# Expert weights queued layer by layer, and a scratch tile taken later, in a graph and mixture-of-experts kernel

## The chip, the cores and the metric

The kernel runs on one core of one Trainium2 chip. The metric is device microseconds for one execution. A core has a matrix engine (TensorE, in the profile PE, with PEld for its weight loads), a vector engine (DVE), a scalar engine (ACT), GpSimd (POOL) and a sync engine (SP) that does nothing here but issue transfers. Transfers run on the core's 16 DMA engines. The engines run side by side and wait for each other by semaphores.

## The reference

Two steps on 1024 nodes of 512 values. The first is a graph layer: normalise, multiply by W, sum over 16384 weighted edges, add a bias, ReLU, add to x. The second is a mixture of 64 experts of which each node takes two, plus a small shared network. Cut to what matters:

```python
x = x + relu(segment_sum(edge_val[:, None] * (layernorm(x) @ W)[edge_col], edge_row) + bias)
xt = layernorm(x)
scores = sigmoid(xt @ Wg.T + bg)
w, idx = top_k(scores, 2);  w = w / w.sum(-1)
cw = zeros(T, E);  cw[t, idx[t]] = w[t]
nx = layernorm(xt)
h = silu(nx @ (gamma*W1) + b1p) * (nx @ (gamma*W3) + b3p)      # per expert, W1 and W3: 512 x 256
y = sum over experts of (h * cw) @ W2 + cw @ b2                # W2: 256 x 512
z = shared network (32 hidden values)
return x + y + z
```

Everything is float32. The weights of one expert are three matrices of 512 KB, so all 64 experts are some 100 MB, and each is read once.

## The kernel before

**The stages.** First comes the graph stage (up to about 170 us): layer norm, product with W, adjacency blocks built from one-hot rows (L402 to L422, L490), their products with the node values (L515), then scores, the choice of two experts per node, and for each expert the list of its nodes (L522 to L629). Then the expert stage: experts are handled in pairs, two blocks of 64 rows side by side. The last part adds results to the nodes and stores them (L1059 to L1086).

**The expert loop** (L999) runs over `order`: 32 pairs, and at index 24 one extra block of 128 rows for an expert that has more than 64 nodes (the index NP in `order`; which expert it is, is known only at run time and read into a register of SP from `oexp_i`). Turn n does, in this order:

- load weights (below); `fetch(n + 4)`: GpSimd gathers the 128 rows of a later pair;
- `hidden` (L771): the first layer, on PE, 8 products over W1 and W3 of both experts (L782, 16 in the trace), then SiLU on ACT (L785) and a multiply on DVE (L787);
- `back(n - 1)`: the second layer of the pair before (`outputs`, L804), copied by ACT and scattered to `y_d` by GpSimd;
- at given turns some side work: at turn 2 `beyond()` (L841), which finds out which experts have more nodes than one block holds; at turns 3 to 11 one-hot rows for the list of the extra blocks (`beyond_hots`, DVE) and, a turn later, their products (`beyond_list`, PE, L910); from turn 6 on, in turns of three, `other_rows` (DVE), `other_turn` (PE) and `other_sum` (PE, DVE) for the shared network and b2;
- `turned` (L794): h is transposed; `front(n + 2)`: the rows of the pair after next are transposed (L194) and scaled (L765, L767).

PE, DVE, ACT, POOL and SP all keep the order in which the program writes their instructions (`manual_schedule`, L988).

**The places for weights.** One pool, `wpool` (L93), has 13 places (AHEAD) of 8 KB a partition under the tag "w13", for W1 and W3 of an expert, and 13 of 4 KB under the tag "w2", for W2. The graph stage uses the same places for its own tiles (`big` and `mid`, L103, L106), and an expert's load waits until the place that it takes is free. Places are handed out as they come free in program order, so that each further W2 takes the place of an earlier W2 or of another tile with that tag. One such other tile is `room` (L843), the scratch of `beyond()`.

**The order on SP's queue.** SP issues loads one after another, and if one must wait, those behind it wait as well. Besides, each load waits for the landing of the load eight before it, so that eight are under way at most. In turns 0 to 2 the loads go expert by expert: W1, W3, W2 (L734, L735, L741). At turn 3 the first layers of experts 6 to 12 are queued together and then their second layers (L1002 to L1006). From expert 13 on it is expert by expert again, except for the last pair, whose first layers precede its second ones (L1011). After all weights, SP loads `ys`, the scattered results, from `y_d` (L1023).

Of the kernel before, what the change touches and what calls it, by code (L numbers as in the profile page):

```python
# [16 lines left out]
ENG = mybir.EngineType  # L17
# [1 line left out]
P = 128  # L19
EPS = 1e-5  # L20
AHEAD = 13
EARLY = 6


@with_exitstack
def kernel(
# [44 lines left out]
    nc = tc.nc  # L71
    N, D = x.shape
    NE = src.shape[0]
    E, _, H = W1.shape
    HS = Ws1.shape[1]
    NT = N // P
# [11 lines left out]
    NP = E // 2  # L88
# [17 lines left out]
    def mid(shape, name, dt, bufs=None):  # L106
        return wpool.tile(shape, dt, name=name, tag="w2")
# [30 lines left out]
    EH = E // 2  # L138
    bias3 = const.tile([3 * EH, 2, 2 * H], BF16, name="bias3")
    picks = const.tile([3 * EH, 2, E], BF16, name="picks")  # L140
# [60 lines left out]
    with tc.tile_pool(name="graph", bufs=1) as gp, \  # L201
# [18 lines left out]
        with tc.manual_schedule(engines={ENG.PE, ENG.DVE, ENG.Activation, ENG.Pool}):  # L220

            nc.gpsimd.iota(iota, pattern=[[1, P]], base=0, channel_multiplier=0, allow_small_or_imprecise_dtypes=True)
            early = mid([P, 8, P], "early", F32)
# [507 lines left out]
    def load_first(queue, w1_of, w3_of):  # L731

        w13 = wpool.tile([P, 2, KC, H], F32, name="w13", tag="w13")
        queue.dma_start(w13[:, 0], w1_of.rearrange("o (p k) h -> p (o k) h", k=KC))  # L734
        queue.dma_start(w13[:, 1], w3_of.rearrange("o (p k) h -> p (o k) h", k=KC))  # L735
        return w13

    def load_second(queue, w2_of):

        w2 = wpool.tile([P, HC, D], F32, name="w2", tag="w2")  # L740
        queue.dma_start(w2, w2_of.rearrange("o (p c) d -> p (o c) d", c=HC))  # L741
        return w2

    def load_expert(queue, w1_of, w3_of, w2_of):
        return load_first(queue, w1_of, w3_of), load_second(queue, w2_of)
# [77 lines left out]
    either = {a: pick_o[:, a, :] for a in range(2)}  # L823
    novf_i = const.tile([1, 1], I32, name="novf_i")
    oexp_i = const.tile([1, NOVF], I32, name="oexp_i")
# [69 lines left out]
    def beyond_hots(c):  # L895

        hots = []
        for n in range(2):
            so = bp.tile([P, P], F32, name="oso", bufs=2)
            nc.vector.tensor_scalar(so, rank_at, oslot[:, c, n:n + 1], None, op0=ALU.is_equal)  # L900
            bo = bp.tile([P, NOVF], F32, name="obo", bufs=2)
            nc.vector.tensor_scalar(bo, iota[:, :NOVF], block[:, c, n:n + 1], numb[:, c, n:n + 1],
                                    op0=ALU.is_equal, op1=ALU.mult)
            hots.append((so, bo))
        return hots
# [7 lines left out]
    def beyond_lists():  # L913
        nc.vector.tensor_copy(lists_o, found)
        nc.vector.tensor_scalar(tokens_o, lists_o, 1, None, op0=ALU.logical_shift_right)
# [51 lines left out]
    order = list(range(NP))  # L967
    order.insert(NP - 8, NP)
    LAST = NP
    xTs, hTs = {}, {}  # L970

    def fetch(n):
        if n < len(order):
            q = order[n]
            gather(rows_of[n % NR], tokens[:, q:q + 1] if q < NP else tokens_o[:, 0:1])

    def front(n):
        if n < len(order):
            q = order[n]
            g, b = (gT[:, :, 2 * q:2 * q + 2], bT[:, :, 2 * q:2 * q + 2]) if q < NP else (g_o, b_o)  # L980
            xTs[n] = scaled(rows_of[n % NR], g, b)

    def back(n):
        if n >= 0:
            q = order[n]
            scatter(outputs(*hTs.pop(n)), lists[:, q:q + 1] if q < NP else lists_o[:, 0:1])

    with tc.manual_schedule(engines={ENG.PE, ENG.DVE, ENG.Activation, ENG.Pool, ENG.SP}):  # L988
        for rows in rows_of:
            nc.scalar.activation(rows, ones[:, 0:1].to_broadcast([P, D]), AF.Copy, scale=0.0)  # L990
        for n in range(NR):
            fetch(n)
        front(0)
        fetch(NR)
        front(1)

        hots, st, sT = None, None, None
        loaded = {}
        for n, q in enumerate(order):  # L999
            if q < NP:  # L1000
                both = (2 * q, 2 * q + 1)
                if n == EARLY // 2:  # L1002

                    early = range(EARLY, AHEAD)
                    firsts = [load_first(nc.sync, W1[e:e + 1], W3[e:e + 1]) for e in early]
                    loaded = {e: (w13, load_second(nc.sync, W2[e:e + 1])) for e, w13 in zip(early, firsts)}  # L1006
                if n < LAST:
                    experts = [loaded.pop(e) if e in loaded else
                               load_expert(nc.sync, W1[e:e + 1], W3[e:e + 1], W2[e:e + 1]) for e in both]
                else:  # L1010
                    experts = list(zip([load_first(nc.sync, W1[e:e + 1], W3[e:e + 1]) for e in both],  # L1011
                                       [load_second(nc.sync, W2[e:e + 1]) for e in both]))
                parts = [(of, {e // EH: picks[:, e // EH, e:e + 1]}) for of, e in zip(experts, both)]
            else:
                e = nc.values_load(oexp_i[0:1, 0:1], engines=[ENG.SP], min_val=0, max_val=E - 1)
                parts = [(load_expert(nc.sync, W1[ds(e, 1)], W3[ds(e, 1)], W2[ds(e, 1)]), either)]
            fetch(n + 4)
            if n == LAST:

                y_of = y_d.rearrange("(i p n) d -> i p n d", p=P, n=2)  # L1020
                ys = [wpool.tile([P, 2, 2, D], F32, name="ys", tag="w13")[:, j] for i in range(NT // 2) for j in range(2)]
                for i in range(NT):
                    nc.sync.dma_start(ys[i], y_of[i])  # L1023
                hots_last = [block_hots(tokens[:, NP - 2 + m:NP - 1 + m], w_last[m]) for m in range(2)]
                diag = wpool.tile([P, 2, P], F32, name="diag", tag="w2")
                for j in range(2):
                    nc.scalar.activation(diag[:, j, :], ident, AF.Copy, scale=wts[:, NT - 2 + j, 1:2])
            h = hidden(xTs.pop(n), parts)
            if n < LAST:
                back(n - 1)  # L1030
            else:
                y_last = [outputs(*hTs.pop(LAST - 1))]
            if n == 0:
                weights()
            if n == 2:
                beyond()
            if 4 <= n < 4 + NT:
                beyond_list(hots)
            if 3 <= n < 3 + NT:
                hots = beyond_hots(n - 3)  # L1040
            if n == 4 + NT:
                beyond_lists()

            if n >= 6 and (n - 6) // 3 < NT:
                i = (n - 6) // 3
                if n % 3 == 0:
                    st = other_rows(i)
                elif n % 3 == 1:
                    sT = other_turn(st)
                else:  # L1050
                    other_sum(i, sT)
            if n == LAST - 2:
                w_last = [block_weights(lists[:, NP - 2 + m:NP - 1 + m]) for m in range(2)]
            hTs[n] = (turned(h), parts)
            front(n + 2)

        pos = {}

        def add_block(m, i):  # L1059
            if m == 0:  # L1060
                pos[i] = psx.tile([P, D], F32, name=("xpt", "xph", "xpy", "xpht")[i % 4])
            nc.tensor.matmul(pos[i], hots_last[m][:, i, :], y_last[m], start=(m == 0), stop=(m == 1))  # L1062
            if m == 0 and i >= NT - 2:
                nc.tensor.matmul(pos[i], diag[:, i - NT + 2, :], ys[i][:, 1, :], start=False, stop=False)

        def add_rows(i):
            for n in range(2 if i < NT - 2 else 1):
                nc.vector.scalar_tensor_tensor(res[:, i, :], ys[i][:, n, :], wts[:, i, n:n + 1], res[:, i, :],
                                               op0=ALU.mult, op1=ALU.add)

        def add_sums(i):
            nc.vector.tensor_add(res[:, i, :], res[:, i, :], pos.pop(i))
            queues[i % 2].dma_start(out[i * P:(i + 1) * P, :], res[:, i, :])

        queues = (nc.scalar, nc.sync)
        add_block(0, 0)
        y_last.append(outputs(*hTs.pop(LAST)))
        add_block(0, 1)
        for i in range(2):
            add_rows(i)  # L1080
        for i in range(NT):
            add_block(1, i)
            if i + 2 < NT:
                add_block(0, i + 2)
                add_rows(i + 2)
            add_sums(i)  # L1086
        more = nc.values_load(novf_i[0:1, 0:1], min_val=1, max_val=NOVF)


    with tc.For_i(1, more, 1) as m:  # L1090
        e = nc.values_load(oexp_i[0:1, ds(m, 1)], engines=[ENG.Activation, ENG.DVE], min_val=0, max_val=E - 1)
        experts = load_expert(nc.scalar, W1[ds(e, 1)], W3[ds(e, 1)], W2[ds(e, 1)])
        of = bp.tile([P, 1], I32, name="otok", bufs=1)
# [6 lines left out]
        parts = [(experts, either)]  # L1100
# [39 lines left out]
```

## Time and profile before

| what | value |
|---|---|
| runs | 449.75, 448.04, 450.18 us; median 449.75 |
| profiled execution | 449.39 us |
| its span (first to last recorded instruction) | 447.6 us |
| PE busy | 400.4 us (89%) |
| DVE, ACT, POOL busy | 243.6, 117.3, 121.9 us |
| moved by DMA | 132.49 MB, mean 296 GB/s |
| mean granted clock of TensorE | 0.96 |
| products of the first layer, L782 | 520, together 130.2 us |
| products of the second layer, L804 | 260, together 68.5 us |

How to read it: the profile is of one execution on the core. Busy shares are of the whole span, while the kernel has stages with different limits, so the prediction reads single stretches of it. A matmul of L782 or L804 is recorded with some 0.59 us, but these overlap: 16 of L782 take 3.60 us. The bandwidth in 40 slices of 11.2 us shows the stages, from the start of the span:

```profile
GB/s 258 99 116 99 152 350 102 399 369 53 203 102 142 90 370 297 31 213 413 406 407 407 407 408 407 407 408 409 406 406 409 408 407 404 408 409 407 244 312 94
```

The slices from the 19th to the 37th, some 201 to 414 us, are the weights.

### The profile page before, as it was taken

What the parts mean: (1) busy time and instruction counts of PE and PEld (TensorE: products, weight loads), DVE (VectorE), ACT (ScalarE), POOL (GpSimd) and SP (SyncE); (2) the same over time, 40 slices, a digit from 0 to 9 for tenths busy, and PEclk for the clock granted to TensorE, in tenths of its full rate; (3) what the DMA queues carried; (4) which work ended last, traced back from release to release, by engine and by line L of the source; (5) the groups of instructions that cost most, each with busy time, mean ns of one, the idle gap of its engine ahead of it and who ended that gap; (6) DMA issues with size and microseconds to landing.
All of it is one profiled execution on the core that took longest, in us unless ns stands there. A gap on an engine that the chain in (4) does not pass through costs nothing.

```text
span 447.6 us, 6352 instructions
## 1 busy us (share of the span) xinstructions
PE 400.4 (89%) x2130; PEld 191.6 (43%) x2130; DVE 243.6 (54%) x723; ACT 117.3 (26%) x241; POOL 121.9 (27%) x162
## 2 busy tenths in 40 slices
PE   2999769988999963797999999999999999899993
PEld 1554545645555542332444444344343444334441
DVE  4869899548677773429435444243333242231782
ACT  1235799332222221111121222122122121211200
POOL 5450800003333334322223232232313233212100
PEclk9999999988999975898899999999999999999999
DMA  8377492991524297169999999999999999999672
GB/s 258 99 116 99 152 350 102 399 369 53 203 102 142 90 370 297 31 213 413 406 407 407 407 408 407 407 408 409 406 406 409 408 407 404 408 409 407 244 312 94
DMA packets 40982, 132.49 MB, mean 296 GB/s; under 512 B 7116, under 2 KB 7260, under 8 KB 40816
## 3 DMA queue, kind: packets, MB, share of 16 engines
q1 hardware_dynamic: 31040, 109.66, 62.4%
q0 software_dynamic: 9184, 20.28, 15.2%
q10 hardware_dynamic: 720, 2.10, 1.2%
q8 instruction: 18, 0.29, 0.3%
q14 instruction: 20, 0.16, 0.1%
HBM read 124.13 MB, written 18.62 MB: 319 GB/s over the span
## 4 chain that ended last, share of the span: by engine, by line
DMA 41%; PE 34%; DVE 7%; ACT 4%; issue 1%; POOLq 0%; ACTq 0%; SPq 0%; DVEq 0%
DMA w<-in_L_ffn_W_dram 40%; PE acc L515 12%; PE xph L782 7%; PE xpy L804 3%; ACT ov L418 2%; PE ph L496 2%; PE ph L564 2%; PE pt L508 1%; PE pt L194 1%; ACT A L501 1%; PE xpt L1062 1%; PE xph L1062 1%; PE xpht L1062 1%; PE xpy L1062 1%; DMA rows<-nx_d,tokens 1%
## 5 line engine op out<-in xcount | busy, mean ns | idle before, releaser
L782 PE MATMUL xph<-w,xT 128*64 128x512 f32 (+1 forms) x520 | 130.2, 610 | 3.1 <-DMA w<-in_L_ffn_W_dram 3.0
L811 POOL DMA_INDIRECT y_d<-xy,lists x30 | 31.6, 1052 | 148.7 <-DMA y_d<-xy,lists 43.4
L782 PEld LDWEIGHTS xph<-w,xT 128*64 128x64 f32 (+1 forms) x520 | 42.2, 141 | 69.0 <-issue 65.1
L804 PE MATMUL xpy<-w,xhT 128*64 128x512 f32 (+1 forms) x260 | 68.5, 594 | 0.0
L787 DVE TENSOR_TENSOR xh<-xa,xph 128x256 f32<-128x256 f32 x33 | 13.9, 421 | 97.8 <-ACT xa L785 97.8
L515 PE MATMUL acc<-hw,AT 128*128 128x512 f32 x128 | 62.5, 615 | 0.4 <-ACT AT L509 0.4
L785 ACT ACTIVATE xa<-xph 128x256 f32<-128x256 f32 x33 | 12.7, 384 | 130.7 <-PE xph L782 130.7
L753 POOL DMA_INDIRECT rows<-nx_d,tokens x32 | 34.0, 1062 | 16.0 <-issue 7.9
L804 PEld LDWEIGHTS xpy<-w,xhT 128*64 128x64 f32 (+1 forms) x260 | 21.4, 138 | 37.6 <-issue 35.8
L765 DVE TENSOR_TENSOR xT<-xpt,gT 128x512 f32<-128x512 f32 x32 | 22.0, 688 | 18.7 <-PE xpt L194 18.4
L308 PE MATMUL ph<-w_sb,hT 128*128 128x512 f32 x64 | 31.6, 642 | 0.7 <-ACT hT L301 0.7
L807 ACT COPY xy<-xpy 128x512 f32<-128x512 f32 x33 | 19.3, 585 | 46.0 <-PE xpy L804 46.0
L515 PEld LDWEIGHTS acc<-hw,AT 128*128 128x128 f32 x128 | 22.6, 196 | 17.4 <-issue 16.8
L194 PE MATMUL xpt<-ident,rows 128*128 128x128 f32 x132 | 22.2, 295 | 4.8 <-DMA rows<-nx_d,tokens 4.8
L547 POOL DMA_DIRECT2D nx_d<-row x8 | 4.5, 560 | 77.6 <-ACT row L546 77.6
L418 ACT CAST ov<-eq 128x1536 f32<-128x1536 bf16 x16 | 24.7, 1547 | 0.0
L767 DVE TENSOR_TENSOR xT<-xT,bT 128x512 f32<-128x512 f32 x32 | 22.2, 692 | 1.1
L496 PE MATMUL ph<-ov,ol 128*32 128x128 f32 x512 | 17.3, 276 | 5.3 <-ACT A L501 5.0
L194 PEld LDWEIGHTS xpt<-ident,rows 128*128 128x128 f32 x132 | 19.1, 211 | 5.1 <-DMA rows<-nx_d,tokens 5.1
L194 PE MATMUL pt<-ident,row 128*128 128x128 f32 x64 | 12.4, 323 | 8.3 <-DVE row L188 2.8
L794 PEld LDWEIGHTS xpht<-ident,xh 128*128 128x128 f32 x66 | 11.8, 212 | 17.9 <-DVE xh L787 8.1
L308 PEld LDWEIGHTS ph<-w_sb,hT 128*128 128x128 f32 x64 | 12.6, 208 | 14.9 <-issue 13.1
(271 smaller groups left out, 508.0 us busy)
## 6 DMA issues: line engine op xcount, KB each, us to landing
w<-in_L_ffn_W_dram SPq DMA_DIRECT2D x195, 512.0 KB, 10.9
y_d<-row POOLq DMA_DIRECT2D x1, 4096.0 KB, 14.6
ys<-y_d SPq DMA_DIRECT2D x8, 512.0 KB, 6.8
base_d<-in_L_gnn_bias_dram POOLq DMA_DIRECT2D x1, 2048.0 KB
row<-base_d POOLq DMA_DIRECT2D x8, 256.0 KB, 8.2
nx_d<-row POOLq DMA_DIRECT2D x8, 256.0 KB, 3.6
w_sb<-in_L_gnn_W_dram ACTq DMA_DIRECT2D x1, 1024.0 KB
res<-in_x_dram SPq DMA_DIRECT2D x2, 512.0 KB, 8.7
```

Of the source, the lines that this page charges most:

```text
L194: nc.tensor.transpose(ps[:, k, :], v[:, k, :], ident[:n, :n])
L308: nc.tensor.matmul(ph, hT[:, k, :], w_sb[:, k, :], start=(k == 0), stop=(k == KC - 1))
L418: nc.scalar.copy(ov[:, :, :VA], eq)
L496: nc.tensor.matmul(pa[LO * w:LO * (w + 1), u, :], ol[:, q, :], ov[:, q, :], start=True, stop=True)
L515: nc.tensor.matmul(accs[t], ATs[h][t // 4][:, t % 4, wq, :], hws[h][:, wq, :], start=(h == 0 and wq == 0), stop=(h == NH - 1 and wq == NQ ...
L753: nc.gpsimd.indirect_dma_start(out=rows, out_offset=None, in_=nx_d[:, :], in_offset=bass.IndirectOffsetOnAxis(ap=of, axis=0), bounds_check ...
L765: nc.vector.tensor_tensor(xT.rearrange(view, n=n), pt.rearrange(view, n=n), g[:, :, :, None].to_broadcast(over), ALU.mult)
L767: nc.vector.tensor_tensor(xT.rearrange(view, n=n), xT.rearrange(view, n=n), b[:, :, :, None].to_broadcast(over), ALU.add)
L782: nc.tensor.matmul(ph[n * r:(n + 1) * r], xT[:, k, n * r:(n + 1) * r], w13[:, :, k, :], start=False, stop=(k == KC - 1))
L804: nc.tensor.matmul(py[n * r:(n + 1) * r], hT[:, c, n * r:(n + 1) * r], w2[:, c, :], start=(c == 0), stop=(c == HC - 1))
L807: nc.scalar.copy(y, py)
L811: nc.gpsimd.indirect_dma_start(out=y_d[:, :], out_offset=bass.IndirectOffsetOnAxis(ap=numbers, axis=0), in_=y, in_offset=None, bounds_chec ...
```

## The change

It does three things.

1. The two layers have loads of their own. `load_until(layer, end)` queues the loads of one layer up to the block number `end`. `units` lists the 65 blocks in the order of use, `at[n]` is the number of blocks before turn n. At turn 0 the first six blocks are queued layer by turns, as before. Then each turn n queues first layers up to `at[n] + 13` and after them second layers up to `at[n - 1] + 13`. The first layers of a turn are those whose places hidden(n - 1) has left, the second layers those whose places outputs(n - 2) has left. So from turn 2 on the queue reads: two first layers, two second layers, and the first layers are two blocks ahead of the second ones.
2. `beyond()`, with its tile `room`, moves from turn 2 to turn 6 (BEYOND), and with it the lists of the extra blocks: `beyond_hots` to turns 7 to 14, `beyond_list` to turns 8 to 15, `beyond_lists` to turn 16.
3. The register with the extra block's expert is read where the loads of that block are queued, which is now at turn 18 instead of 24.

In the program as built, the places turn out as follows. Before, `room` took the place of an early graph tile (`b13`), W2 of experts 6 to 11 took the last graph tiles, and W2 of expert 12 took the place of W2 of expert 0. Now W2 of experts 6 to 12 all take graph tiles (that of expert 12 the row tile that expert 11 had), `room` takes the place of W2 of expert 10, and W2 of expert 24 takes the place of `room`. The order of first-layer places is the same in both. The numbers of instructions on PE, DVE, ACT and POOL are the same.

```diff
-EARLY = 6
...
+    BEYOND = 6
     xTs, hTs = {}, {}
+    units = [e for q in order for e in ((2 * q, 2 * q + 1) if q < NP else (None,))]
+    at = [sum(2 if q < NP else 1 for q in order[:n]) for n in range(len(order) + 1)]
+    experts = [[None, None] for _ in units]
+    EARLY = 6
+    loaded = [0, 0]
+    beyond_e = []
+
+    def of(w, e):
+        return w[e:e + 1] if e is not None else w[ds(beyond_e[0], 1)]
+
+    def load_until(layer, end):
+        for u in range(loaded[layer], min(end, len(units))):
+            e = units[u]
+            if e is None and not beyond_e:
+                beyond_e.append(nc.values_load(oexp_i[0:1, 0:1], engines=[ENG.SP], min_val=0, max_val=E - 1))
+            experts[u][layer] = load_second(nc.sync, of(W2, e)) if layer else load_first(nc.sync, of(W1, e), of(W3, e))
+            loaded[layer] = u + 1
...
-        loaded = {}
         for n, q in enumerate(order):
-            if q < NP:
-                both = (2 * q, 2 * q + 1)
-                if n == EARLY // 2:
-
-                    early = range(EARLY, AHEAD)
-                    firsts = [load_first(nc.sync, W1[e:e + 1], W3[e:e + 1]) for e in early]
-                    loaded = {e: (w13, load_second(nc.sync, W2[e:e + 1])) for e, w13 in zip(early, firsts)}
-                if n < LAST:
-                    experts = [loaded.pop(e) if e in loaded else
-                               load_expert(nc.sync, W1[e:e + 1], W3[e:e + 1], W2[e:e + 1]) for e in both]
-                else:
-                    experts = list(zip([load_first(nc.sync, W1[e:e + 1], W3[e:e + 1]) for e in both],
-                                       [load_second(nc.sync, W2[e:e + 1]) for e in both]))
-                parts = [(of, {e // EH: picks[:, e // EH, e:e + 1]}) for of, e in zip(experts, both)]
-            else:
-                e = nc.values_load(oexp_i[0:1, 0:1], engines=[ENG.SP], min_val=0, max_val=E - 1)
-                parts = [(load_expert(nc.sync, W1[ds(e, 1)], W3[ds(e, 1)], W2[ds(e, 1)]), either)]
+            if n == 0:
+                for u in range(EARLY):
+                    load_until(0, u + 1)
+                    load_until(1, u + 1)
+            load_until(0, at[n] + AHEAD)
+            load_until(1, at[max(n - 1, 0)] + AHEAD)
+            parts = [(experts[u], either if units[u] is None else {units[u] // EH: picks[:, units[u] // EH, units[u]:units[u] + 1]})
+                     for u in range(at[n], at[n + 1])]
             fetch(n + 4)
...
-            if n == 2:
+            if n == BEYOND:
                 beyond()
-            if 4 <= n < 4 + NT:
+            if 2 <= n - BEYOND < 2 + NT:
                 beyond_list(hots)
-            if 3 <= n < 3 + NT:
-                hots = beyond_hots(n - 3)
-            if n == 4 + NT:
+            if 1 <= n - BEYOND < 1 + NT:
+                hots = beyond_hots(n - BEYOND - 1)
+            if n == BEYOND + 2 + NT:
                 beyond_lists()
```

## The prediction

> **What bounds the kernel now.** All times are from the start of the span. I call one 512 KB weight transfer a load; there are 195 (W1, W3, W2 of 65 blocks), numbered as SP issues them. "hidden(n)" is the first-layer product of pair n (L782), "outputs(n)" the second (L804).
>
> I read the stretches of the expert phase first: busy time of PE, PEld, DVE, ACT, POOL, then granted clock, DMA share, GB/s.
>
> ```profile
> 170.00:175.00 5.00, 1.26 (x6) 0.97 (x6) 2.55 (x15) 0.00 (x1) 0.53 (x1) 0.50 0.98 397
> 175.00:180.00 5.00, 2.09 (x10) 1.59 (x10) 0.89 (x2) 0.00 (x0) 3.31 (x4) 0.50 0.37 107
> 180.00:185.00 5.00, 4.94 (x18) 1.67 (x16) 1.79 (x3) 0.00 (x0) 1.31 (x2) 0.73 0.18 50
> 185.00:190.00 5.00, 2.74 (x16) 1.39 (x16) 2.66 (x9) 2.04 (x3) 1.17 (x2) 1.00 0.01 3
> 190.00:195.00 5.00, 5.00 (x28) 2.04 (x26) 0.44 (x3) 1.21 (x3) 0.94 (x1) 1.00 0.24 34
> 195.00:200.00 5.00, 5.00 (x26) 1.60 (x24) 1.80 (x3) 0.41 (x2) 2.07 (x2) 1.00 0.98 323
> ```
>
> The transfer engines stand nearly idle from 175 to 194, then are full from 195 until the weights end near 417. Why they stand idle is in SP's waits between 160 and 200:
>
> ```profile
> SPq L741 <- PE xpy L804: 22.6, 1, 22.6
> ```
>
> One second-layer load, that of expert 12 (load 39), stands at the head of SP's queue until outputs(0) is done; SP issues it at 194.07, with first-layer loads queued behind it.
>
> The chain that ended last puts 40% of the span on weights. That overstates it, so I read PE's order of time. Early pairs run without any wait for weights, late ones don't:
>
> ```profile
> 279.09 3.60 PE L782 MATMUL xph<-w,xT 128*64 128x512 f32 x16
> 285.57 3.60 PE L782 MATMUL xph<-w,xT 128*64 128x512 f32 x16
> 292.82 3.60 PE L782 MATMUL xph<-w,xT 128*64 128x512 f32 x16
> 299.23 3.60 PE L782 MATMUL xph<-w,xT 128*64 128x512 f32 x16
> ...
> 385.38 3.19 PE L782 MATMUL xph<-w,xT 128*64 128x512 f32 x13 [1.32 <-DMA w<-in_L_ffn_W_dram]
> ...
> 394.01 3.19 PE L782 MATMUL xph<-w,xT 128*64 128x512 f32 x13 [1.11 <-DMA w<-in_L_ffn_W_dram]
> ```
>
> Undisturbed, hidden starts follow each other by 6.41, 6.48 or 7.25 us (the latter two with a transpose or a product of the other rows). From pair 23 on they take longer: 23 to 24 1.18 over, 26 to 27 0.95, 27 to 28 0.93, 28 to 29 2.36, 29 to 30 2.16, 30 to 31 0.52, 31 to 32 1.57 (7.50 against 5.93, as no transpose of rows follows), and 0.45 of stretch in hidden(32). Sum 10.1 us: what late weights cost. Before 23 they cost nothing. The other loss is beyond(), the work on blocks past the first of an expert, at pair 2:
>
> ```profile
> 202.41 0.22 PE L861 MATMUL xpy<-ident,oexp 128*1 128x31 f32 x2 [1.83 <-DVE oexp L859]
> ...
> 204.08 4.87 PE L782 MATMUL xph<-w,xT 128*64 128x512 f32 x16
> ...
> 212.31 0.51 PE L794 MATMUL xpht<-ident,xh 128*128 128x128 f32 x2 [1.65 <-DVE xh L787]
> ...
> 213.48 5.29 PE L782 MATMUL xph<-w,xT 128*64 128x512 f32 x16
> ```
>
> L794 at 193.97 to L794 at 220.88 is 26.91 us for three pairs, against 3 x 6.41 + 0.46 (one L910 group): 7.2 us lost to two gaps and two slow products.
>
> **What the Trainium skill says.** "Perfetto Trace Analysis", Optimization Strategy: kernels can have regimes with different most-contended engines, and interleaving them can help. The trace agrees: transfers idle at 175 to 194, PE short of weights after 345. "DMA: Bandwidth & Descriptors", Issuing engines are not separate DMA queues: loads from SP and gathers from GpSimd run on the same 16 engines; here a load takes 1.46 us while gathers and scatters run beside it ((385.38 - 194.07) / 131, load 170 ending the wait at 385.38). "TensorE: Matmul & The Clock Gate", What's actually happening: the clock is halved by an idle window of about 3.4 us. Here gaps of 1.83 and 1.65 us sufficed for 0.50 in the next 2 to 3 us; the measurement decides.
>
> **The change part by part.**
>
> 1. The room leaves the turn between W2 of experts 5 and 6. Each of experts 6 to 12 now gets a W2 place from the graph stage; expert 12 gets the row tile that expert 11 had, free at 171.06. Load 39 moves from 194.07 to about 171, behind a backlog that ends at 174.8: that end becomes about 176.1. The first gather (issued 174.47, landed 177.9, PE waits for it) meets it. Bounds 0 (the queues share by turns) and 1.3 us (it stands behind the load); I take +0.4.
>
> 2. First layers go ahead. Loads 40 to 43 (experts 13, 14) need hidden(0), ended at 185.3; 44 to 47 need hidden(1), 192.3; two W2 need outputs(0), 194.0. Later groups of six follow hidden(n-1) every 6.4 us, while serving six takes 8.8, so the engines stay full from 192.3. Load 44 would have gone at 194.07 + 5 x 1.46 = 201.4; it now goes at 192.3. Every load is 9.1 us earlier.
>
> 3. Order of what is left. With firsts two blocks ahead of seconds, hidden(32) needs the 192nd load instead of the 193rd, hidden(31) the 187th instead of the 188th, hidden(29) the 173rd instead of the 176th. outputs(n) needs its W2 later than before by up to six loads (8.8 us), but the advance covers that early, and at the end the last W2 is the 195th either way.
>
> 4. beyond() moves to pair 6. DVE's 9.95 us of it (200.62 to 210.55) and PE's gaps stay as they were: 7.2 us again. But pair 6 also has other_rows(0) on DVE, 235.72 to 237.11, now between beyond() and the multiply that PE waits for: +1.4. The eight list products go with it to pairs 8 to 15, costing the same, but three of them instead of two now precede an L943 product, which waits 0.28 for their sum: +0.3.
>
> 5. The room's wait. It takes a place of the W2 ring then, and W2 of expert 24 (load 79) takes that place when DVE has left it: outputs(5) at about 226.1 plus 8.95 (200.45 to 209.4), 235. Each load is issued when the eighth before it has landed; load 79 is served at 192.3 + 2.3 (first flight) + 35 x 1.46 = 245.7, so SP reaches it some 11.7 earlier, at 234. So the queue stands for 1 to 3 us with some seven loads, 10 us, under way: nothing. Queued behind it are the first layers of experts 27 on, which land near 250 and are used at pair 13, past 279.
>
> 6. Reading the extra block's expert on SP moves from turn 24 to 18. Before it fits between issues at 336.32 and 337.57; with eight loads under way it costs nothing, uncovered about 1 us. Nothing else on PE, ACT or POOL changes in number.
>
> Sum. PE alone: hidden(32) really starts at 415.71 + 0.45 = 416.2; minus 10.1, plus 0.4 + 1.4 + 0.3, is 408.2. Weights alone: load 193 came at 416.2, 192 some 1.3 sooner (spacing (409.77 - 394.01) / 12), minus 9.1: 405.8. hidden(31): PE 402.2, weights 408.5 - 9.1 = 399.4; hidden(29): 388.5 against 381. So PE is last everywhere, by 2.4 us at the least, and the tail after hidden(32) (31.4 us, PE's products with ys one after another) moves along: ys wait for the scatter of pair 30, which moves by the same amount, and DVE has 1.89 us to spare at 439.38. Gain 8.0: span 439.6, execution 449.39 - 8.0 = 441.4. The profiled execution is 0.36 under the median, so 441.6.
>
> **The rivals.**
>
> A, as summed, PE bound throughout: 441.6, 439.5 to 443.7. For it the regular pairs up to 345; against it a margin of only 2.4 us. 0.60.
>
> B, weights stay last: a thinner advance, say 5 instead of 9.1 (a drained queue at 192 and slower loads beside gathers). hidden(32) at 414.9 - 5 = 409.9 to 412: 443.3 to 445.5, I say 444.7. For it DMA at full share for 220 us; against it the count of loads. 0.17.
>
> C, the stall at pair 6 costs more: if the gap, now about 3 us, holds the clock at half for another product (3.44 us more work time), 445.0. For it 0.50 after shorter gaps; against it only the first 2 to 3 us were slow. 0.10.
>
> D, no change: PE's regular pairs get longer where it no longer waits, or the gain is eaten by both B and C: about 449. Against it 130 us at clock 1.00 from 220 to 350 with no gap. 0.06.
>
> E, slower: SP's one queue stands at load 79 while the room is in use. The loads under way last until about 245; every us after that delays all 116 later ones. With 2.4 us of margin, 8.0 of gain and 2.2 to be told from no change, it decides once the room is left later than 257.6, 22 us after my estimate; at 262 the time is 454. Against it, the same work took 8.95 us at pair 2. 0.07.
>
> **How the numbers follow.** About 0.5% (2.2 us) is what can be told from no change: under 447.5 lie A, B, C: 0.87; same, D: 0.06; slower, E: 0.07. The range holds A, C, nearly all of B and, below, a beyond() that hides better (its two slow products, 1.3 and 1.7 us, gone): 438.6 to 446.6.
>
> **What would show it.** Right: DMA share high already in 185 to 195, no L741 wait of 20 us; hidden starts 6.4 to 7.3 us apart to the end, with no waits for weights after pair 23; the slow pair at about 224 to 243 instead of 200 to 219; hidden(32) near 408. Wrong: waits for w at L782 or L804 after 380 (B), half clock over more than two products (C), a DMA share below 0.9 between 236 and 260 (E), a first gather that lands after 179.

## The result and the profile after

The changed kernel takes 446.46 us (median), the kernel before 448.47 us in the same series: a ratio of 0.9952, interval 0.9933 to 0.9971. The gain is 2.0 us where 8 were forecast. The profiled execution of the changed kernel has a span of 444.7 us against 447.6 us.

The stretches of the expert phase of the changed kernel: busy time of PE, PEld, DVE, ACT, POOL, then granted clock, DMA share, GB/s.

```profile
175.00:180.00 5.00, 4.12 (x14) 2.38 (x16) 2.67 (x4) 0.00 (x0) 2.00 (x2) 0.50 0.20 55
180.00:185.00 5.00, 3.94 (x14) 1.26 (x10) 0.00 (x0) 0.98 (x1) 0.00 (x0) 0.78 0.10 26
185.00:190.00 5.00, 3.79 (x22) 1.86 (x24) 2.67 (x9) 1.06 (x3) 2.11 (x2) 1.00 0.81 315
190.00:195.00 5.00, 5.00 (x28) 2.03 (x26) 1.75 (x3) 1.24 (x3) 1.04 (x1) 1.00 0.57 157
195.00:200.00 5.00, 5.00 (x28) 1.99 (x26) 0.47 (x2) 1.22 (x3) 1.03 (x1) 1.00 0.89 312
200.00:205.00 5.00, 5.00 (x27) 1.65 (x26) 1.80 (x3) 0.41 (x2) 2.04 (x2) 1.00 1.03 417
```

The hole in the transfers is partly filled: 315 GB/s at 185 to 190 where there were 3. But 190 to 195 is only 0.57 full and 195 to 200 only 0.89. They are full from 200 on, not from 192.3. The 22.6 us wait at a second-layer load is gone; in its place SP now stands 15.6 us at the first layer of expert 13 (L733), whose place hidden(0) has to leave.

PE's order of time at the moved `beyond()`, and then at the last pairs:

```profile
226.68 0.22 PE L860 MATMUL xpy<-ident,oexp 128*1 128x31 f32 x2 [1.83 <-DVE oexp L858]
...
227.99 3.60 PE L781 MATMUL xph<-w,xT 128*64 128x512 f32 x16
236.33 3.29 PE L803 MATMUL xpy<-w,xhT 128*64 128x512 f32 x8 [4.74 <-ACT xhT L795]
...
400.87 4.07 PE L781 MATMUL xph<-w,xT 128*64 128x512 f32 x15
...
407.68 4.00 PE L781 MATMUL xph<-w,xT 128*64 128x512 f32 x15
...
417.61 0.70 PE L793 MATMUL xpht<-ident,xh 128*128 128x128 f32 x2 [3.79 <-DVE xh L786]
418.11 1.91 PE L1072 MATMUL xpt<-xy,bhots 128*128 128x512 f32 x2
419.95 2.48 PE L803 MATMUL xpy<-w,xhT 128*64 128x512 f32 x8
```

Two things are to be seen. Hidden(31) and hidden(32), at 400.87 and 407.68, show no wait of PE for weights, though each is stretched (4.07 and 4.00 for 15 products, where 16 take 3.60). The list of waits has one for the weight loads of PE at hidden(31): PEld stands 0.71 us for `w`. And there is a wait that was not there before: 3.79 us ahead of the transpose of the last block, after which the next products run slow.

Hidden(0) to hidden(32) took 180.55 to 415.71 before, 235.16 us; it takes 178.43 to 407.68 now, 229.25: 5.9 us gained. From hidden(32) to the end of the span it was 31.9 us and is 37.0: 5.1 us given back. With the wait for the first rows, 1.1 us longer, nothing is left: from the issue of the first row gather to the end these two profiles take 273.1 us before and 273.5 now. So they show where time was gained and lost, but not the 2.0 us by which the medians differ; in which part those arise is not shown.

The chain that ended last says by whom the 5.1 us are taken (start, time, what):

```profile
401.11 6.12 DMA y_d<-xy,lists
407.23 0.02 issue
407.25 0.02 ACTq L806
407.26 0.04 issue
407.30 0.59 ACT xy L806
407.90 0.08 issue
407.97 0.98 POOL y_d L810
...
409.34 3.15 DMA bw<-w_d,lists
...
412.57 2.14 DVE bhots L960 x8
...
415.09 2.14 DVE bhots L960 x8
417.23 0.34 DVE xh L786
```

Read upwards. The multiply xh that PE waits for stands on DVE behind the two `bhots` groups (L960, from `block_hots`). These wait for `bw`, the weights of the last two blocks' rows, which `block_weights` (L949) gathers on GpSimd. The gathers are queued at turn 30, behind a scatter of y (L810), and that scatter waits until the one before has landed, 6.12 us. The copy of xy on ACT (L806) that stands between two scatters in the chain is not what the second one writes out. There are two xy tiles; the copy at 407.30 fills, for pair 30, the tile that the landing has freed, while the scatter at 407.97 writes out pair 29, copied at 400.41. From a landing to the next scatter about 0.75 us pass, with such a copy between (407.23 to 407.97) or without (378.59 to 379.36).

GpSimd's order of time shows the same queue from its own side:

```profile
394.20 1.02 POOL L810 DMA_INDIRECT y_d<-xy,lists  x1 [5.62 <-ACT xy L806]
401.11 0.99 POOL L810 DMA_INDIRECT y_d<-xy,lists  x1 [5.88 <-ACT xy L806]
407.97 0.98 POOL L810 DMA_INDIRECT y_d<-xy,lists  x1 [5.87 <-ACT xy L806]
...
409.34 1.04 POOL L949 DMA_INDIRECT bw<-w_d,lists  x1 [0.27 <-POOL bw L948]
...
410.77 1.02 POOL L949 DMA_INDIRECT bw<-w_d,lists  x1 [0.27 <-DMA y_d<-xy,lists]
```

In the kernel before, GpSimd's order of time and then PE's at the last block:

```profile
408.02 0.98 POOL L811 DMA_INDIRECT y_d<-xy,lists  x1 [6.78 <-ACT xhT L796]
...
409.38 1.05 POOL L950 DMA_INDIRECT bw<-w_d,lists  x1 [0.27 <-POOL bw L949]
...
410.82 1.02 POOL L950 DMA_INDIRECT bw<-w_d,lists  x1 [0.27 <-POOL bw L949]
...
421.67 0.50 PE L794 MATMUL xpht<-ident,xh 128*128 128x128 f32 x2
```

The gathers went at 409.38 and 410.82 before and go at 409.34 and 410.77 now: PE comes earlier, GpSimd doesn't. Before, the transpose of the last block (L794) stands in PE's order without a wait. How far each scatter's issue lies behind the end of the product outputs(n) that it writes out (both from the orders of time, us):

```
pair n            15    20    24    27    29
before           2.7   6.5   5.7   1.4   0.9
changed          1.0   4.9   6.6   8.1   8.2
```

From pair 20 to pair 29 the changed kernel's scatters follow each other by 6.7 to 7.1 us beside full weight traffic, with two steps of 8 (there the landing took 7.37 and 7.20 us; why is not shown), and PE's pairs by 6.4 to 7.3. On average that is 7.11 us for a scatter, 6.84 without the two long steps, and 6.74 for a pair. So the queue, once behind, doesn't catch up. Before, late weights slowed PE from pair 23 on, and that let GpSimd catch up.

### The profile page after: what moved, and what is told of

It is laid out like the page before. It is cut to its first block, busy times and chain, and to the rows that moved or that the text cites. A ratio compares the mean times of both kernels' runs of the same rounds, so it can differ in the third digit from the quotient of the medians.

```text
span 444.7 us, 6426 instructions
## 1 busy us (share of the span) xinstructions
PE 391.5 (88%) x2130; PEld 185.0 (42%) x2130; DVE 243.8 (55%) x723; ACT 117.2 (26%) x241; POOL 122.0 (27%) x162
## 4 chain that ended last, share of the span: by engine, by line
PE 59%; DMA 13%; DVE 9%; ACT 5%; issue 2%; POOL 0%; POOLq 0%; ACTq 0%; DVEq 0%
PE xph L781 18%; PE acc L514 11%; DMA y_d<-xy,lists 10%; PE xpy L803 9%; PE xpt L193 3%; ACT ov L417 2%; PE ph L495 2%; PE xpht L793 2%; PE xph L777 2%; PE pt L507 1%; PE ph L563 1%; DMA y_d<-xy,lists_o 1%; PE xpy L942 1%; ACT A L500 1%; PE xpy L909 1%
## 5 line engine op out<-in xcount | busy, mean ns | idle before, releaser
L781 PE MATMUL xph<-w,xT 128*64 128x512 f32 (+1 forms) x520 | 122.5, 600 | 0.1
L810 POOL DMA_INDIRECT y_d<-xy,lists x30 | 31.1, 1037 | 145.3 <-ACT xy L806 53.7
L803 PE MATMUL xpy<-w,xhT 128*64 128x512 f32 (+1 forms) x260 | 66.0, 610 | 4.7 <-ACT xhT L795 4.7
L781 PEld LDWEIGHTS xph<-w,xT 128*64 128x64 f32 (+1 forms) x520 | 38.7, 139 | 62.2 <-issue 58.4
L514 PE MATMUL acc<-hw,AT 128*128 128x512 f32 x128 | 60.7, 600 | 0.4 <-ACT AT L508 0.4
L803 PEld LDWEIGHTS xpy<-w,xhT 128*64 128x64 f32 (+1 forms) x260 | 19.4, 141 | 45.0 <-issue 39.4
L806 ACT COPY xy<-xpy 128x512 f32<-128x512 f32 x33 | 19.3, 585 | 49.8 <-PE xpy L803 44.1
L793 PEld LDWEIGHTS xpht<-ident,xh 128*128 128x128 f32 x66 | 11.8, 212 | 20.8 <-DVE xh L786 12.7
L793 PE MATMUL xpht<-ident,xh 128*128 128x128 f32 x66 | 15.1, 311 | 6.0 <-DVE xh L786 6.0
```

The lines of the kernel that those rows point to most:

```text
L514: nc.tensor.matmul(accs[t], ATs[h][t // 4][:, t % 4, wq, :], hws[h][:, wq, :], start=(h == 0 and wq == 0), stop=(h == NH - 1 and wq == NQ ...
L781: nc.tensor.matmul(ph[n * r:(n + 1) * r], xT[:, k, n * r:(n + 1) * r], w13[:, :, k, :], start=False, stop=(k == KC - 1))
L793: nc.tensor.transpose(pt[:, c, :], v[:, c, :], ident)
L803: nc.tensor.matmul(py[n * r:(n + 1) * r], hT[:, c, n * r:(n + 1) * r], w2[:, c, :], start=(c == 0), stop=(c == HC - 1))
L810: nc.gpsimd.indirect_dma_start(out=y_d[:, :], out_offset=bass.IndirectOffsetOnAxis(ap=numbers, axis=0), in_=y, in_offset=None, bounds_chec ...
```

## The experiments

Theory S: the scatters and, behind them, the gathers of `block_weights` set the tail. Rivals: the stall at pair 6 eats the gain (B), or weights stay late (W). These letters are those of the experiments: B here is rival C of the prediction, and W is its rival B. Each group of four ran on one chip with the kernel before beside it; every ratio is to that, with its 95% interval. Line numbers are those of the changed kernel.

**The gathers moved, in three ways.** First to turn 12, where GpSimd's queue is hardly behind:

```diff
-            if n == LAST - 2:
+            if n == 12:
                 w_last = [block_weights(lists[:, NP - 2 + m:NP - 1 + m]) for m in range(2)]
```

> The changed kernel with block_weights, the two small gathers (bw) of the last two pairs' weights, moved from turn 30 to turn 12 on GpSimd; nothing else. Theory S (the scatters of y, each waiting on GpSimd for the landing of the one before, hold bw back, and bw holds the DVE work ahead of the last transpose): bw lands long before, the 6.0 us DVE wait for bw and the 3.8 us PE wait for xh of the last block go, and the time falls by 2 to 4 us against the changed kernel (446.5), to 442.5 to 444.5; not by all 5 us that the tail lost, as ys still wait for the last scatter. Theory W (late weights still set the end): no change, 446 to 447. Theory B (the stall at pair 6 ate the gain): no change either.

441.81 us, ratio 0.9826 (0.9800 to 0.9852). A second time, with the third group:

> The change with block_weights at turn 12 once more, as the one the other three are compared with on the same chip: 440.5 to 443, no wait of PE for w in the last pairs.

443.12 us, ratio 0.9851 (0.9815 to 0.9887). Moving two gathers gives about five of the six missing microseconds, more than the 2 to 4 that were expected. DVE's wait for `bw` is gone. The waits of DVE from 395 us on, second time:

```profile
DVE res L1078 <- DMA ys<-y_d: 6.6, 2, 5.8
```

Now DVE waits for `ys`, which wait for the last scatter: S is one step further down the same queue. The same edit one turn later than in the change, with `LAST - 1` in place of `LAST - 2`:

> The changed kernel with block_weights one turn later (31 instead of 30), so that one more scatter stands ahead of bw. Theory S: bw goes out after the scatter of pair 30 and lands 2 to 4 us later than in the changed kernel, and the end moves by as much: 448.5 to 450.5. Theories W and B: no change, 446 to 447.

452.29 us, ratio 1.0082 (1.0053 to 1.0112): a loss, larger than expected. Its waits of DVE from 395 us on:

```profile
DVE bhots L960 <- DMA bw<-w_d,lists: 10.8, 2, 9.1
```

The same edit in the kernel before, where weights are last:

> The kernel before with block_weights moved to turn 12. Theory S: there the last block comes about 6 us later after the start of the experts, and bw (issued at 409.4 and 410.8) has landed before it is wanted, so nothing changes: within 1 us of the kernel before (448.5). If the reads of bw were a cost of their own, it would get faster by 2 us or more.

448.11 us, ratio 0.9984 (0.9965 to 1.0004). Nothing that can be told, as S has it: before, the gathers arrived while PE was held by weights anyway. So it is neither the cheaper queue nor the turn itself that pays, but only the wait that the change brought out.

**The scatters taken apart.** The results of every second pair go to a buffer of their own, `y_e`, so that a scatter no longer waits for the one before (these results are missing from the output):

```diff
+    y_e = dram.tile([2 * N, D], F32, name="y_e")
...
-            scatter(outputs(*hTs.pop(n)), lists[:, q:q + 1] if q < NP else lists_o[:, 0:1])
+            scatter(outputs(*hTs.pop(n)), lists[:, q:q + 1] if q < NP else lists_o[:, 0:1], y_e if n % 2 else y_d)
```

> The changed kernel with the scatters of every second pair going to a second buffer in memory that nobody reads, so that a scatter doesn't wait for the one just before it; the results of every second pair (odd index in the order) are left out of the output. Transfers and work are the same in number. Theory S: GpSimd no longer lags, the chain of scatters at 6 us each goes, bw lands near 403, ys come some 3 us earlier, and the time falls by 4 to 6 us against the changed kernel, to 440.5 to 442.5, near what the prediction had. Theory W: 446 to 447. Theory B: 446 to 447.

441.02 us, ratio 0.9813 (0.9787 to 0.9839), with the gathers left at turn 30; they go at 401.46 and 402.91, some 8 us sooner. Both together:

> The change with block_weights at turn 12 and the scatters of every second pair in a buffer of their own (their results are left out of the output). Theory S2: ys no longer wait 5.6 us for the lagging scatters, 1 to 2 us below the same with one buffer, 439.5 to 441. If PE alone bounds: no difference, 440.5 to 442.5.

441.77 us, ratio 0.9812 (0.9779 to 0.9845), against 0.9851 for the moved gathers alone on that chip. The intervals overlap, so it is not settled what the wait for `ys` is still worth. Nor do the two edits add up: together they give no more than the second buffer alone. In its profile the weights are next, with PEld standing 2.0 us for `w` in the last pairs.

**One part of the change alone.** The layer order, with the room left at pair 2:

```diff
-    BEYOND = 6
+    BEYOND = 2
```

> The layer order alone, with the room left at pair 2. The room now takes the place of a used second layer, so W2 of expert 12 still gets a graph tile and the advance stays. The stall of beyond() should fall from 8.9 us at pair 6 to about 7.2 us at pair 2, so hidden(32) comes 1 to 2 us sooner than in after. Theory S (GpSimd's scatters and the gathers of block_weights set the tail): no gain from that, bw lands at about the same time, 445.5 to 447.5. Theory B (the stall at pair 6 is what ate the gain): 1.7 us gained, 444 to 445. Theory W (late weights): 446.5 or more, with waits for w in the last pairs.

444.66 us, ratio 0.9919 (0.9884 to 0.9954). The median meets B's figure, yet its profile is not B's alone: the stall is shorter, the scatter of pair 29 is 5.1 us behind and not 8.2, so `bw` is late by only 0.9 us, and weights hold PE for 2.4 us at hidden(31). The profile is of an execution of 442.73 us, 1.9 under the median, so its short tail need not be the usual one. Its interval touches that of the change, so a gain over it is not shown. The place of the room alone, with the old order of layers (an edit of the kernel before; the lists of the extra blocks follow four turns later too):

```diff
-            if n == 2:
+            if n == 6:
                 beyond()
```

> The place of the room alone, with the layers ordered as before. Load 39 no longer waits for outputs(0), but W2 of expert 13 does, with two of its first layers ahead of it: three loads of 1.46 us advance, 4.4 us. hidden(32) by weights then at about 412 instead of 416, with small waits for w. Theory S: the tail waits for bw in any case, which lands at about 412.5, so the end is near that of after: 446 to 448. Theory W (the order is what counts, and weights bound it): 447.5 to 449. If the pair-6 stall shows in full: 449 to 450.5.

448.06 us, ratio 0.9984 (0.9958 to 1.0010): nothing that can be told. PE waits for weights there as W said, in a profiled execution of 444.80 us. So the layer order alone gains what can be told from no change, and the place of the room alone does not; how the 2.0 us of the change divide between them is not settled, as the intervals touch.

**Is the stall at pair 6 still to be had?** With the gathers at turn 12, the room at pair 5, where no `other_rows` follows, and at pair 2:

> The change with block_weights at turn 12 and beyond() at pair 5, where no other_rows stands behind it. Theory S with the pair-6 stall's own cost: ACT's Silu no longer holds up the copy of xhT, 1.5 to 2 us less than with block_weights alone moved: 439.5 to 441. Theory that the stall costs the same wherever it is (its gap and the half clock): 441.5 to 442.5. If the wait for ys, which come behind the scatters, bounds the tail: 441 to 442, with a longer wait of PE or DVE for ys.

> The layer order with the room left at pair 2, and block_weights at turn 12. Theory S with the pair-6 stall's own cost: 1.5 to 2 us below the change with block_weights alone moved, 439.5 to 441. If the wait for ys bounds the tail: 441 to 442, though hidden(32) comes sooner. Theory that the place of the room is needed for the advance: 445 or more, with waits for w in late pairs.

442.97 us, ratio 0.9874 (0.9836 to 0.9913), and 443.30 us, ratio 0.9882 (0.9849 to 0.9915). The 1.5 to 2 us did not come. With the room at pair 5 the chain that ended last runs, from 377 us on, through the scatters one after another, the loads of `ys` and DVE. With the room at pair 2 it runs through the weights. PE's order of time there:

```profile
398.69 1.02 PE L781 MATMUL xph<-w,xT 128*64 128x512 f32 x2
402.09 4.91 PE L781 MATMUL xph<-w,xT 128*64 128x512 f32 x13 [2.38 <-DMA w<-in_L_ffn_W_dram]
...
409.75 3.60 PE L781 MATMUL xph<-w,xT 128*64 128x512 f32 x16
```

PE arrives sooner at hidden(31), waits 2.38 us for its third product's weights, and then runs 13 products in 4.91 us where 13 took 3.19 in the kernel before. The stretch is the clock's: granted were 0.61, 0.50, 0.50 and 0.69 in the four microseconds from 403 on, and 1.00 before the wait. So the late weights cost about 4 us here, not 2.4. To test that late weights are the cause, the three loads of expert 20 are left out, 1.5 MB, and its products use the weights of expert 19:

```diff
+            if e == 20:
+                experts[u][layer] = experts[u - 1][layer]
+            else:
+                experts[u][layer] = load_second(nc.sync, of(W2, e)) if layer else load_first(nc.sync, of(W1, e), of(W3, e))
```

> Layer order, room left at pair 2, block_weights at turn 12, and the three loads of expert 20 left out (its products use expert 19's weights): 4.4 us of transfers less. Theory W2 (with the stall shortened, late weights of the last two pairs are the floor, and that is why the room at pair 2 won nothing): no wait for w at pair 31, hidden(32) near 404.5 instead of 409.75, 438 to 440. Theory S2 (the lag of the scatters and the wait for ys are the floor): hidden(32) earlier, but PE or DVE waits for ys, 441.5 to 443.

440.62 us, ratio 0.9778 (0.9745 to 0.9810), against 0.9882 with all loads. The same place in its profile:

```profile
400.81 3.60 PE L781 MATMUL xph<-w,xT 128*64 128x512 f32 x16
...
406.74 3.60 PE L781 MATMUL xph<-w,xT 128*64 128x512 f32 x16
...
426.58 1.13 PE L1077 MATMUL xpy<-ys,diag 128*128 128x512 f32 x2 [1.21 <-DMA ys<-y_d]
```

No wait for weights and no stretch: up to hidden(32) the late weights were what held PE. Further on PE waits 1.21 us for `ys`, and DVE 5.1 us, which is what S2 had expected; the time lies between the ranges of W2 and S2. The same loads left out where the room stays at pair 6:

> The change with block_weights at turn 12 and the loads of expert 20 left out. PE comes later here by the stall at pair 6, and so just meets the weights: theory W2 gains nothing or at most 0.5 us against the same with all loads, 440 to 442.5. If weights bound this version too: 438 to 439.5.

440.34 us, ratio 0.9784 (0.9753 to 0.9815), against 0.9851 on the same chip: 3.0 us, where nothing was expected, though the two intervals just touch. PE gains nothing by it up to hidden(32) (227.56 us from hidden(0), against 228.89 with all loads, where hidden(1) ran 1.70 slower, at a granted clock down to 0.50). The tail is shorter: 30.9 us from hidden(32) to the end, against 33.2. GpSimd's order of time with the three loads left out:

```profile
405.76 0.98 POOL L810 DMA_INDIRECT y_d<-xy,lists  x1 [5.67 <-DMA y_d<-xy,lists]
410.75 1.05 POOL L810 DMA_INDIRECT y_d<-xy,lists  x1 [4.01 <-DMA y_d<-xy,lists]
```

and with all of them:

```profile
408.01 0.98 POOL L810 DMA_INDIRECT y_d<-xy,lists  x1 [5.64 <-ACT xy L806]
412.59 0.98 POOL L810 DMA_INDIRECT y_d<-xy,lists  x1 [3.59 <-DVE xh L786]
```

The last two scatters go about 2 us sooner, though hidden(0) starts 1.7 us later, and `ys` at 413.23 instead of 415.00. My expectation counted only PE's weights; the transfers left out also let the scatters go sooner.

This limits what the run before it shows. With the three loads left out, 440.62 us with the room at pair 2 and 440.34 at pair 6 are the same: even where no weights are late, the room at pair 2 wins nothing. PE gains 2.1 us by it up to hidden(32) (225.48 us from hidden(0), against 227.56) and loses 1.3 in the tail (32.3 us, against 30.9), where `ys` are waited for. So late weights are one floor and the scatters with `ys` the next, close behind.

Of the versions that leave nothing out, the change with the gathers at turn 12 has the lowest ratios, 0.9826 and 0.9851 in its two series, and beats both kernels. Those with the room at pair 5 or 2 besides can't be told from it.

## Why the prediction was wrong, point by point

**Load 39 and the first gather.** Right in kind. PE waits 5.9 us for the first rows where it waited 4.8, 1.1 more against 0.4 with bounds 0 to 1.3; with the gathers at turn 12 it waits 5.27 and 5.56. Hidden(0) takes 5.52 instead of 4.75 here, as the granted clock stays at 0.50 until 182 us. That is not shown to come from the longer gap: after the gap of 5.56 it took 4.36.

**The advance of the loads.** Mis-sized. I had 9.1 us from an engine full from 192.3 on. SP's order of time has load 68 at 221.90 instead of 228.40 and the last issue at about 401.7 instead of 408.4: 6.5 and 6.7 us. Hidden(1) ended 1.4 us earlier in this execution for reasons ahead of it, so 10.5 would have been needed. The missing 4 us are for the most part at 190 to 200: from 191 on, full engines would have moved 9 x 407 = 3,660 KB; the stretches show at most (157 + 312) x 5 = 2,345 KB, 3.2 us short. SP had only the four first-layer loads of one pair to issue at a time: four at 183.94 to 185.27, four at 190.99 to 193.09, two second layers at 195.28, and the next four from 197.40 on.

**The margin of 2.4 us over the weights** was therefore used up: hidden(31) to (32) takes 6.81 instead of 5.93, 0.88 more, of which 0.71 is PEld's wait for `w`. The 15 products of hidden(32) take about 0.6 too long as well, with no wait for weights listed. This is rival B in small.

**beyond() at pair 6.** Right: L793 at 218.24 to L793 at 254.93 is 36.69 us for four pairs whose regular times, two list products among them, come to 27.75, so 8.9 lost where I had 7.2 + 1.4; the 0.3 for a third wait of a list product came besides, 0.28 at 291.05. But the way is another one than a later DVE alone. ACT's order of time:

```profile
235.79 0.23 ACT L928 ACTIVATE sact<-s 128x32 f32<-128x32 f32 x1 [10.44 <-DVE s L926]
235.92 0.35 ACT L795 COPY xhT<-xpht 128x256 f32<-128x256 f32 x1
```

ACT, which works in order, stood 10.44 us at the activation for `other_rows`, with the copy of xhT that outputs(6) needed behind it. The transposes that it copies had been done at about 227.3. PE stood 4.74 us for that copy and then ran outputs(6) in 3.29 us instead of 1.88, at a granted clock of 0.50. The gap of 1.83 us just before left the clock at 1.00, so that a gap of this length is enough for half clock, as the prediction read from pair 2 of the kernel before, doesn't hold everywhere.

**Room and register.** Right: no run shows a cost of either; SP's list of waits has none for DVE between 150 and 400 us beyond 0.4 us, and those are for other lines than the room's.

**hidden(32).** 5.9 us gained from hidden(0) on, where 8.0 were summed (7.95 from start to start, with the 0.4 ahead of hidden(0) put back and the 0.45 inside hidden(32) taken off). Of the 2.05 missing, 0.77 is hidden(0)'s clock, 0.88 the late weights and 0.3 the stall at pair 6. That hidden(32) starts at 407.68, near the forecast 408, is luck: hidden(0) came 2.1 us sooner in this execution, for reasons ahead of the change.

**The step that failed** is the last one: "the tail after hidden(32) (31.4 us, PE's products with ys one after another) moves along". Counted from the recorded start of hidden(32), it was 31.9 us and became 37.0. I checked what `ys` wait for, found a scatter, and let it move with PE: "the scatter of pair 30, which moves by the same amount". It doesn't: hidden(32) moved from 415.71 to 407.68, this scatter only from 416.01 to 413.07, for the scatters form a queue of their own, with a period about PE's; and "Nothing else on PE, ACT or POOL changes in number" looked at counts, not at who had only been on time because PE was late. The gathers of `block_weights` stood in that queue, and DVE's `bhots`, ahead of xh, waited for them. The row of before in the table above held the warning: 6.5 us behind at pair 20 and 5.7 at pair 24, and 0.9 at 29 only after the weights had slowed PE. Moving those gathers gave back 1.0 to 1.3% of the time, and with them moved the forecast of 441.6 us is about met (441.81 and 443.12), though not term by term: up to hidden(32) those profiles gain 6.4 and 6.3 us and not 8, and their tails are 33.2 to 33.3 us long.

That 446.46 lies just inside the range, 438.6 to 446.6, is luck too: its upper end was drawn for rivals B and C, not for a queue of scatters. Two sums are off without consequence: 449.75 less 8.0 is 441.75 and not 441.6, and by its own terms a room left at 262 us gives about 456 and not 454.

**The rivals.** A's PE bound holds for the pairs, not for the tail. B holds in small. Of C's extra cost nothing is seen: the stall took 8.9 us where 8.6 were in the sum. The times of B, C and D (444.7, 445.0, 449) are all nearer to the measured one than mine, but by other mechanisms. E did not come.

## What to carry to other kernels

When a late resource is brought forward, list every queue that was on time only because of it, and compare its own period with the new pace: here a queue of dependent scatters with a period of 6.7 to 7.1 us did not catch up beside pairs of 6.4 to 7.3 us once it was behind. A small transfer whose inputs are ready early should not be queued at the end behind such a queue; here its move was worth more than the change itself. Where several limits lie close together, as PE, the weights and the scatters do here, what one edit gains is bounded by the next limit, and gains of single edits don't add (0.9851 for the gathers moved, 0.9813 for a second buffer, 0.9812 for both).

## What the runs showed of the hardware

A scatter issued on GpSimd took 5.9 to 7.4 us to land beside full weight traffic in the changed kernel (5.91, 6.12, 7.20 and 7.37 among the late pairs); the one issued at 413.07, after the weights, released the `ys` loads at 415.53, so at most 2.5 us later.

In the profiled execution of the kernel before, the granted clock was 0.83 at 97 to 108 us and 0.62 at 108 to 112; in that of the changed kernel it was 1.00 in both stretches. The change touches nothing there, and all of the 3 us between the two spans lies ahead of the first row gather (issued 174.47 and 171.22). Over all fourteen profiles of this case the first row gather is issued at 171.0 to 174.7 us. Two single profiles would thus have shown a gain that belongs to no part of the change.

The gap of 3.79 us ahead of the last block was followed by groups of 1.91 and 2.48 us, which take 1.12 and 1.94 in the version with the gathers at turn 12 and the room at pair 2. The granted clock was 0.50 from 418 to 421 us and 1.00 before the gap. So that wait cost its own length and 1.3 us of slow products as well.
